# Expert feed-forward: first product of experts 2 to 6 by seven block products in place of eight

## The chip, the cores and the metric

The kernel runs on one core of one Trainium2 chip. A core has five engines with their own instruction queues: PE (TensorE, matrix products), ACT (ScalarE), DVE (VectorE), POOL (GpSimd) and SP (SyncE, which here only starts transfers). PE writes its results to PSUM, of which this stage has eight banks of 128 x 512 floats; ACT and DVE read PSUM, POOL doesn't. Each engine takes its instructions in order and waits on semaphores for the others.

The metric is the device time of one execution in microseconds. Three runs of the kernel before gave 1509.0, 1509.32 and 1512.29 us: median 1509.32. The profile shown is of one more execution, which took 1511.89 us around a span of 1510.1 us from its first instruction to its last.

## The reference, cut to what matters

The model has two layers on 4096 tokens of 256 values in float32. The change lies in the last part, an expert-choice mixture: each of eight experts takes the 1024 tokens that score highest for it, runs them through two matrix products, and adds the result, scaled, to those tokens.

```python
S = sigmoid(xt @ Wg).T                     # 8 x 4096
G, I = top_k(S, 1024)                      # of each expert
ex = xt[I]                                 # 8 x 1024 x 256
hid = gelu(einsum('ekh,ehf->ekf', ex, W1) + b1[:, None, :], approximate=False)
out = (einsum('ekf,efh->ekh', hid, W2) + b2[:, None, :]) * G[..., None]
new_x = zeros_like(xt).at[I.reshape(-1)].add(out.reshape(-1, h))
x = x + layernorm(new_x)
```

W1 is 256 x 1024 for each expert and W2 is 1024 x 256. The first product is thus 1024 tokens x 256 x 1024, with all three sizes even in halves: 2 x 512 tokens, 2 x 128 inputs, 2 x 512 hidden values.

## The kernel before, in words

The mixture is the last stage of the kernel. It works in 16 units `u` of 512 tokens: expert `e = u // 2`, half `q = u % 2` of its tokens. Unit 0 begins at about 1020 us of the profile.

**One unit.** `turn(u, c)` (L2090) transposes the gathered tokens, 128 x 128 at a time, into one PSUM bank (`tp`, two banks) for each half `c` of the 256 inputs, and DVE copies the bank to `xT`. `feed_forward(u)` (L2105) then runs over eight blocks `f` of 128 hidden values: two products of 128 x 128 weights with 128 x 512 tokens (c = 0, 1) add up in one bank `ph` (three banks in turn), and ACT puts the Gelu of it into `hid[:, f, :]` (L2127). Every float32 product is two PE instructions in the profile. Then, for each of four blocks `i` of 128 tokens, eight products give `py` (128 x 256, two banks, L2137). DVE adds the bias to `y` (L2156) and multiplies by the gate (L2157), and POOL starts an indirect transfer that adds the 128 rows of `y` to the tokens' rows in memory, `acc_d` (L2158). There are four `y` buffers. After `i` = 1 and 2 the unit transposes half c = 0 and 1 of the next unit's tokens.

**Weights.** Two experts' weights are held. `load_expert(e + 2)` (L1712) is called when expert e is through: SP loads w1 when the last product that reads the old w1 is done, and w2 likewise.

**The order.** The order of the PE, DVE and ACT instructions is the order in which the program writes them (`manual_schedule`, L1692). POOL's is found by the scheduler up to unit 12, and from there on (L2202) it too is the written one. Transfers that add to `acc_d` are ordered one behind the other, since they write the same tensor; only those of expert 6 are declared independent of each other (`beside_each_other`, L1956).

**The lists.** Which 1024 tokens an expert takes is found while earlier experts run. Searches for the thresholds (of expert 0, of 1, of 2 and 3 together, of 4 to 7 together: a `compare` and ten `tick` each, L1750 and L1764) and the experts' lists (`sort`, `rank`, `chunks`, `places`, `collect`, `gather`, L1877) stand in an agenda. `go_on_with_lists(u, time)` (L2182) is called after each `f` and each `i`; it takes `time` from what the last step is reckoned to cost, and issues the next step when less than 0.3 is left and the step's `behind` allows it. A `gather` makes eight indirect transfers of 128 tokens on POOL (L1928).

**The end.** Before unit 13 POOL is given eight fetches of the last expert's residual rows, `xg` (L2204). Before unit 14 `begin_last` (L2043) reads the sums `acc_d` back: SP brings six blocks of 512 tokens, POOL fetches the last expert's own rows `accg`, both when all transfers of expert 6 have landed. Beside units 14 and 15 the sums of the eight blocks are normalized (statistics on DVE, the power on POOL, L1973, scaling on ACT, L1993) and written out, and at the end the last expert's tokens are written over them by eight transfers (L2032), which wait for all blocks to have been written.

The tiles `x0` to `x3` (128 x 1024 floats each) hold tokens of the first layers, and the mixture doesn't read them before the change.

Of the kernel before, what the change touches and what calls it, by code (L numbers as in the profile page):

```python
# [9 lines left out]
F32 = mybir.dt.float32  # L10
# [9 lines left out]
P = 128  # L20
D = 256
DC = D // P
TB = 512
# [51 lines left out]
def kernel(  # L75
# [1613 lines left out]
    with ExitStack() as st4:  # L1689
# [400 lines left out]
        def turn(u, c, half=None):  # L2090

            if c == 0 and not half:
                xT[u] = wk.tile([P, DC, TB], F32, tag="xT", name="xT")
            e, q = divmod(u, QPE)
            tiles = range(NJ) if half is None else range(half * NJ // 2, (half + 1) * NJ // 2)
            tp = ps.tile([P, NJ, P], F32, tag="tp", name="tp")
            for i in tiles:
                nc.tensor.transpose(tp[:, i, :], lists[e].got[q * NJ + i][:, c * P : (c + 1) * P], ident)  # L2098
                if u == 0 and c == 0 and i == 0:

                    keep_busy(first, 4)
            cols = slice(tiles[0] * P, (tiles[-1] + 1) * P)
            nc.vector.tensor_copy(xT[u][:, c, cols], tp.rearrange("p j t -> p (j t)")[:, cols])  # L2103

        def feed_forward(u):  # L2105
            e, q = divmod(u, QPE)
# [4 lines left out]
            for h in range(TB // n):  # L2111
# [3 lines left out]
                for f in range(FC):  # L2115
                    if not u and not h and f in (FC - 4, FC - 3):
                        turn(0, f - FC + 4, 1)
                    ph = ps.tile([P, n], F32, tag="mm", name="ph", bufs=3)
                    for c in range(DC):
                        nc.tensor.matmul(  # L2120
                            ph,
                            lhsT=w1[:, c, f * P : (f + 1) * P],
                            rhs=xT[u][:, c, h * n : (h + 1) * n],
                            start=(c == 0),
                            stop=(c == DC - 1),
                        )
# [5 lines left out]
                    aside(u, "f", f)  # L2132
            for i in range(NJ):
                k = q * NJ + i
                py = ps.tile([P, D], F32, tag="y", name="py")
                for f in range(FC):
# [4 lines left out]
                        start=(f == 0),  # L2141
                        stop=(f == FC - 1),
                    )
                if u == 1:
                    if i == 2:
                        for c in range(DC):
                            turn(u + 1, c)
                elif i in (1, 2) and u + 1 < NE * QPE:
                    turn(u + 1, i - 1)
# [17 lines left out]
                if e == NE - 2:  # L2167

                    beside_each_other(scatter, summed)
                go_on_with_lists(u, 2.3)  # L2170

        searches = [Search(0), Search(1), Search(2, 3), Search(4, 5, 6, 7)]
        agenda = []
        for search in searches[1:]:
            agenda.extend(search.steps())
            for e in search.es:
                agenda.extend(lists[e].steps())
        left = [0.0]  # L2180

        def go_on_with_lists(u, time):  # L2182
            left[0] = max(left[0] - time, 0.0)
            if agenda and left[0] < 0.3 and agenda[0][1] <= u:
                spent, _, step = agenda.pop(0)
                left[0] += spent
                step()

        first = ps.tile([P, TB], F32, tag="mm", name="idle", bufs=3)
# [9 lines left out]
        for u in range(NE * QPE):  # L2199
# [5 lines left out]
                    last.fetch(xg[:, c, :], x_d, c)  # L2205
            elif u == (NE - 1) * QPE:
                begin_last()
            feed_forward(u)
            if q == QPE - 1 and e + 2 < NE:
                weights.append(load_expert(e + 2))  # L2210

# [33 lines left out]
```

## Time and profile before

| what | value |
| --- | --- |
| median of three runs | 1509.32 us (1509.0 to 1512.29) |
| profiled execution | 1511.89 us, its span 1510.1 us, mean clock granted to PE 0.985 |
| mixture from its first `ph` to the last `py` | 1020.7 to 1498.4 us |
| `ph`, L2120, PE | 544 instructions (480 of 128 x 512, 64 of 128 x 256), 229.6 us busy |
| `py`, L2137, PE | 1024 instructions of 128 x 256, 229.7 us busy |
| Gelu from a bank of 128 x 512, L2127, ACT | 120, 687 ns each |
| copy of a bank of 128 x 512 to `xT`, L2103, DVE | 30, 691 ns each |
| `y`, L2156 and L2157, DVE | 56 each, 420 and 364 ns |
| transfers that add to `acc_d`, L2158, POOL | 56, 1586 ns of POOL each |
| transfers that gather tokens, L1928, POOL | 64, 1041 ns of POOL each |

An entry such as `128x512 f32<-128x512 f32` is partitions x elements and type, of the output and of the input. In a timeline the columns are start, duration, engine, line, operation, output <- input, number of instructions and, in brackets, how long the engine stood before it and what ended that. A duration of several PE instructions is that of the row, so the time from one row's start to the next row's start gives the pace.

### The profile page before, as it was taken

The page shows a single profiled execution, that of the slowest core. Times are in us where ns is not written, and L with a number is a line of the kernel's source. Part 1 is how long each engine was busy: PE and PEld are TensorE (multiplying, and loading weights), DVE is VectorE, ACT ScalarE, POOL GpSimd, SP SyncE. Part 2 cuts the span into 40 slices and gives each one's busy share as a digit, 9 for nine tenths or more (in the row PEclk, how much of TensorE's full clock was granted, in tenths as well). Part 3 has the DMA queues.
Part 4 walks back from the last instruction along what each step waited for, and adds up shares of the span by engine and source line. Part 5 has one row for each costly group of instructions (what it writes and reads, how often), then busy time and mean ns, then how long its engine had stood idle before and what let it go on. Part 6 is the DMA issues. An engine that isn't in the chain of part 4 may idle for free. (4 is left out here: it accounts for less than half of the span.)

```text
span 1510.1 us, 24181 instructions
## 1 busy us (share of the span) xinstructions
PE 1461.7 (97%) x9286; PEld 786.1 (52%) x9286; DVE 876.1 (58%) x2140; ACT 698.2 (46%) x1148; POOL 496.5 (33%) x627
## 2 busy tenths in 40 slices
PE   8999999999899999999999999949999999999996
PEld 4666666667532333332333335517666656665674
DVE  5456654666356599659974877775545631322145
ACT  4244455443456666767676788612211122112143
POOL 4123332222350214322432233413334243242554
PEclk9999999999999999999999999969999999999998
DMA  9400000003324141533154210241324324233364
GB/s 219 132 1 1 1 1 1 1 0 101 103 93 144 52 135 60 179 102 102 47 174 140 71 57 30 75 133 34 101 54 92 67 53 98 50 78 81 64 171 122
DMA packets 91885, 121.58 MB, mean 81 GB/s; under 512 B 24925, under 2 KB 64250, under 8 KB 91642
## 3 DMA queue, kind: packets, MB, share of 16 engines
q1 hardware_dynamic: 70000, 73.09, 15.4%
q0 software_dynamic: 21712, 46.94, 13.3%
q8 instruction: 73, 1.20, 0.3%
q14 instruction: 42, 0.34, 0.1%
q10 hardware_dynamic: 58, 0.01, 0.0%
HBM read 66.90 MB, written 53.12 MB: 79 GB/s over the span
## 5 line engine op out<-in xcount | busy, mean ns | idle before, releaser
L1529 PE MATMUL po<-w,vaug 128*17 128x512 f32 (+1 forms) x2304 | 270.1, 551 | 2.8 <-DVE turned L1579 2.6
L2127 ACT ACTIVATE hid<-ph,mb 128x512 f32<-128x512 f32 (+1 forms) x136 | 89.9, 662 | 340.4 <-PE ph L2120 247.8
L2120 PE MATMUL ph<-xT,w 128*128 128x512 f32 (+1 forms) x544 | 229.6, 574 | 0.3 <-DVE xT L2103 0.3
L2137 PE MATMUL py<-w,hid 128*128 128x256 f32 x1024 | 229.7, 380 | 0.0
L2137 PEld LDWEIGHTS py<-w,hid 128*128 128x128 f32 x1024 | 191.7, 190 | 31.7 <-issue 6.7
L1517 DVE TENSOR_SCALAR w<-sc 128x1024 f32<-128x1024 f32 x152 | 185.1, 1222 | 36.2 <-PE sc L1501 33.8
L1509 ACT ACTIVATE w<-sc 128x512 f32<-128x512 f32 x256 | 152.9, 597 | 113.7 <-ACT w L1513 49.5
L1501 PE MATMUL sc<-q,kT 32*128 32x512 f32 (+1 forms) x2304 | 190.8, 413 | 2.2 <-ACT w L1509 1.0
L1501 PEld LDWEIGHTS sc<-q,kT 32*128 32x128 f32 x2304 | 86.2, 183 | 174.7 <-ACT w L1509 92.1
L2158 POOL DMA_INDIRECT acc_d<-y,idx x56 | 88.8, 1586 | 225.2 <-DVE y L2157 103.2
L2120 PEld LDWEIGHTS ph<-xT,w 128*128 128x128 f32 x544 | 99.8, 190 | 107.4 <-issue 98.3
L1513 ACT ACTIVATE w<-sc 128x512 f32<-128x512 f32 x203 | 120.2, 592 | 0.0
L1515 ACT ACTIVATE w<-sc 128x1024 f32<-128x1024 f32 x104 | 106.7, 1026 | 0.0
L2156 DVE TENSOR_TENSOR y<-py,mb 128x256 f32<-128x256 f32 x56 | 23.5, 420 | 126.7 <-PE py L2137 116.1
L1529 PEld LDWEIGHTS po<-w,vaug 128*17 128x17 f32 x2304 | 41.7, 95 | 95.8 <-issue 72.3
L1928 POOL DMA_INDIRECT got<-tok_d,idx x64 | 66.6, 1041 | 62.9 <-DVE counts L1762 24.5
L2103 DVE COPY xT<-tp 128x512 f32<-128x512 f32 (+1 forms) x34 | 22.2, 659 | 71.1 <-PE tp L2098 62.4
L724 PE MATMUL pg<-nT,wh 128*128 128x512 f32 x128 | 61.4, 612 | 1.5 <-ACT nT L663 1.5
L850 PE MATMUL py<-wo,oT 128*128 128x256 f32 x256 | 61.9, 385 | 0.0
L740 PE MATMUL pv<-wh,nT 128*128 128x512 f32 x128 | 59.7, 592 | 0.0
L850 PEld LDWEIGHTS py<-wo,oT 128*128 128x128 f32 x256 | 47.2, 190 | 17.2 <-issue 9.6
L915 ACT ACTIVATE hid<-ph,vec 128x512 f32<-128x512 f32 x64 | 39.8, 685 | 27.5 <-PE ph L906 27.4
(309 smaller groups left out, 2108.8 us busy)
## 6 DMA issues: line engine op xcount, KB each, us to landing
q<-q_d POOLq DMA_DIRECT2D x16, 1024.0 KB
w<-in_L_ffn_W_dram SPq DMA_DIRECT2D x16, 1024.0 KB
q_d<-parts SPq DMA_DIRECT2D x48, 256.0 KB
kT<-k_d POOLq DMA_DIRECT2D x16, 512.0 KB
k_d<-parts SPq DMA_DIRECT2D x24, 256.0 KB
acc_d<-logits SPq DMA_DIRECT2D x8, 512.0 KB
tok_d<-hg SPq DMA_DIRECT2D x32, 128.0 KB
x<-in_L_attn_x_dram SPq DMA_DIRECT2D x7, 512.0 KB
```

Source lines behind the costliest of these rows:

```text
L850: nc.tensor.matmul(py, lhsT=d["oT"][:, e, :], rhs=wo[:, e, :], start=(e == 0), stop=(e == EC - 1))
L1501: nc.tensor.matmul(sc[:, m * n : (m + 1) * n], lhsT=row["kT"][t][rows, r, (kt + m) * P : (kt + m + 1) * P], rhs=row["q"][qh, t][rows, r, p ...
L1509: nc.scalar.activation(w[:, 0, :], singles[0], AF.Relu)
L1513: nc.scalar.activation(w[:, 1, :], singles[1], AF.Relu)
L1515: nc.scalar.activation(w[:, 2:4, :], pair, AF.Relu)
L1517: nc.vector.tensor_scalar(w[:, 2:4, :], pair, 0.0, None, ALU.max)
L1529: nc.tensor.matmul(po[32 * j : 32 * j + HD + 1, weighed(halves, r)], lhsT=row["v"][:, kt + m, HQ * t + 4 * r + j, :], rhs=w[:, j, m * n : ...
L1928: return nc.gpsimd.indirect_dma_start(out=dst, out_offset=None, in_=rows[:, :], in_offset=self.at_chunk(c), bounds_check=NT - 1, oob_is_er ...
L2120: nc.tensor.matmul(ph, lhsT=w1[:, c, f * P : (f + 1) * P], rhs=xT[u][:, c, h * n : (h + 1) * n], start=(c == 0), stop=(c == DC - 1),)
L2127: nc.scalar.activation(hid[:, f, h * n : (h + 1) * n], ph, AF.Gelu, bias=mb1[:, e * FC + f : e * FC + f + 1])
L2137: nc.tensor.matmul(py, lhsT=hid[:, f, i * P : (i + 1) * P], rhs=w2[:, f, :], start=(f == 0), stop=(f == FC - 1),)
L2158: scatter = nc.gpsimd.indirect_dma_start(out=acc_d[:, :], out_offset=lists[e].at_chunk(k), in_=y, in_offset=None, bounds_check=NT - 1, oob ...
```

## The change

For experts 2 to 6 the first product of both halves of the tokens is made at once, by seven products of blocks in place of eight (the form of Strassen's method that Winograd gave). With the weights' four blocks a (of 128 x 512), the tokens' four blocks b (128 x 512) and sums of them S, T, the seven products are a11 b11, S2 T2, S3 T3, S1 T1, a12 b21, a22 T4 and S4 b22, and the four blocks of the hidden values are sums of these.

- **`weight_sums(e)`**: four additions or subtractions of 128 x 512 on POOL, issued ahead of the `py` of the expert before (for expert 2 ahead of unit 3). S3 takes the place of a21 in w1, the others go to halves of x0 to x3.
- **`token_sums(e, n)`**: four subtractions of 128 x 512 on DVE, after the last transposes of the expert before.
- **`feed_forward_by_seven(e)`**: for each of four blocks f, seven products in four banks. ACT copies the first product to `u2`, DVE makes five additions, and ACT makes four Gelu, three of them from SBUF.
- **`project_back(u, hid)`** is the second half of `feed_forward`, taken out; it runs for both halves of the tokens one after the other, and four `hid` blocks of the two halves are ready at once. Both halves of the next expert's tokens are transposed in the second of them.
- The copies of transposed tokens of experts 2 to 6 go from DVE to ACT.
- `tp` shares the banks of `ph`: five of tag `mm` in place of three and two.
- The agenda: the search for experts 4 to 7 moves ahead of list 3, split around it; `go_on_with_lists` is called 15 times in an expert (7 beside the products, 8 beside `py`) in place of 24, with larger times, and beside the products a step may be held back by `most`.
- The loop over units calls `feed_forward_by_seven(6)`, with both `project_back`, at unit 12. The fetches of `xg` stay written at unit 13 of the loop, and so come behind both halves' `py` and their transfers.

```diff
-            tp = ps.tile([P, NJ, P], F32, tag="tp", name="tp")
+            tp = ps.tile([P, NJ, P], F32, tag="mm", name="tp", bufs=5)
...
-            nc.vector.tensor_copy(xT[u][:, c, cols], tp.rearrange("p j t -> p (j t)")[:, cols])
+            copy = nc.scalar.copy if by_seven(e) else nc.vector.tensor_copy
+            copy(xT[u][:, c, cols], tp.rearrange("p j t -> p (j t)")[:, cols])
+
+        def by_seven(e):
+
+            return 2 <= e < NE - 1
+
+        rooms = [x.rearrange("p j d -> p (j d)")[:, h * TB : (h + 1) * TB] for x in xs[:4] for h in range(2)]
+        seven = dict(zip(("sum0", "T1", "sum1", "T2", "T4", "S1", "S2", "S4"), rooms))
+
+        def weight_sums(e):
+
+            w1, _ = weights[e]
+            (a11, a21), (a12, a22) = ([w1[:, c, h * DFF // 2 : (h + 1) * DFF // 2] for h in range(2)] for c in range(DC))
+            for name, x, y, op in (
+                ("S1", a21, a22, ALU.add), ("S3", a11, a21, ALU.subtract), ("S2", "S1", a11, ALU.subtract),
+                ("S4", a12, "S2", ALU.subtract),
+            ):
+                dst = a21 if name == "S3" else seven[name]
+                nc.gpsimd.tensor_tensor(dst, seven[x] if isinstance(x, str) else x, seven[y] if isinstance(y, str) else y, op)
+
+        def token_sums(e, n):
+
+            (b11, b21), (b12, b22) = ([xT[QPE * e + q][:, c, :] for c in range(DC)] for q in range(QPE))
+            t1, t2, t4 = (seven[name] for name in ("T1", "T2", "T4"))
+            dst, x, y = ((t1, b12, b11), (t2, b22, t1), (b12, b22, b12), (t4, b21, t2))[n]
+            nc.vector.tensor_tensor(dst, x, y, ALU.subtract)
+
+        def turns_within(u):
+
+            e, q = divmod(u, QPE)
+            if u == QPE * NE - 1:
+                return {}
+            turns = {c: (lambda c=c: turn(u + 1, c)) for c in range(DC)}
+            if q == QPE - 1 and by_seven(e + 1):
+                both = [
+                    turns[0], turns[1], lambda: turn(u + 2, 0), lambda: token_sums(e + 1, 0), lambda: turn(u + 2, 1),
+                    *(lambda n=n: token_sums(e + 1, n) for n in (1, 2, 3)),
+                ]
+                return {1: both[0:1], 2: both[1:3], 3: both[3:]}
+            if by_seven(e) and q == 0:
+                return {}
+            return {2: [turns[0], turns[1]]} if u == 1 else {1: [turns[0]], 2: [turns[1]]}
+
+        def feed_forward_by_seven(e):
...
+            HC = FC // 2
+            for f in range(HC):
+                a, b, c, d = (ps.tile([P, TB], F32, tag="mm", name=f"ph{k}", bufs=5) for k in range(4))
+                u2 = seven[f"sum{f % 2}"]
+                c22, c21, c12 = hid[1][:, HC + f, :], hid[0][:, HC + f, :], hid[1][:, f, :]
+                product(a, w1[:, 0, 0:half], b11, True, True, f)
+                nc.scalar.copy(u2, a)
+                product(b, s2, t2, True, True, f)
+                nc.vector.tensor_tensor(u2, u2, b, ALU.add)
+                product(c, s3, t3, True, True, f)
+                nc.vector.tensor_tensor(c22, u2, c, ALU.add)
+                product(d, s1, t1, True, True, f)
+                nc.vector.tensor_tensor(c22, c22, d, ALU.add)
+                product(a, w1[:, 1, 0:half], b21, False, True, f)
+                gelu(0, f, a)
+                if f < HC - 1:
+                    go_on_with_lists(QPE * e, 3.2, 1.5)
+                gelu(1, HC + f, c22)
+                product(c, w1[:, 1, half:DFF], t4, False, True, f)
+                nc.vector.tensor_tensor(c21, u2, c, ALU.add)
+                gelu(0, HC + f, c21)
+                product(d, s4, b22, False, True, f)
+                nc.vector.tensor_tensor(c12, u2, d, ALU.add)
+                gelu(1, f, c12)
+                go_on_with_lists(QPE * e, 3.0)
+            for q in range(QPE):
+                if q == 0 and by_seven(e + 1):
+                    weight_sums(e + 1)
+                project_back(QPE * e + q, hid[q])
...
-                go_on_with_lists(u, 2.3)
+                go_on_with_lists(u, 3.4 if by_seven(e) else 2.3)
...
-            agenda.extend(search.steps())
+            agenda.extend(search.steps() if search is not searches[-1] else ())
             for e in search.es:
                 agenda.extend(lists[e].steps())
+                if e == 2:
+                    agenda.extend(searches[-1].steps()[:4])
+                elif e == 3:
+                    agenda.extend(searches[-1].steps()[4:])
...
-            if agenda and left[0] < 0.3 and agenda[0][1] <= u:
+            if agenda and left[0] < 0.3 and agenda[0][1] <= u and agenda[0][0] <= most:
...
-            feed_forward(u)
+            if u == 3:
+                weight_sums(2)
+            if not by_seven(e):
+                feed_forward(u)
+            elif q == 0:
+                feed_forward_by_seven(e)
             if q == QPE - 1 and e + 2 < NE:
                 weights.append(load_expert(e + 2))
```

More of the change, by code (lines that the diff above doesn't have):

```diff
@@ new lines, in feed_forward_by_seven, with product, gelu @@
+        def feed_forward_by_seven(e):
+            w1, w2 = weights[e]
+            hid = [wk.tile([P, FC, TB], F32, tag="hid", name="hid") for _ in range(QPE)]
+            (b11, b21), (t3, b22) = ([xT[QPE * e + q][:, c, :] for c in range(DC)] for q in range(QPE))
+            t1, t2, t4 = (seven[name] for name in ("T1", "T2", "T4"))
+            half = DFF // 2
+            s3 = w1[:, 0, half:DFF]
+            s1, s2, s4 = (seven[name] for name in ("S1", "S2", "S4"))
+            def product(bank, a, b, start, stop, f):
+                nc.tensor.matmul(bank, lhsT=a[:, f * P : (f + 1) * P], rhs=b, start=start, stop=stop, skip_group_check=not start)
+            def gelu(n, f, src):
+                nc.scalar.activation(hid[n][:, f, :], src, AF.Gelu, bias=mb1[:, e * FC + f : e * FC + f + 1])
+            HC = FC // 2
[27 more added lines that the diff above has]
+                project_back(QPE * e + q, hid[q])
@@ L2117, in feed_forward @@
                         turn(0, f - FC + 4, 1)
-                    ph = ps.tile([P, n], F32, tag="mm", name="ph", bufs=3)
+                    ph = ps.tile([P, n], F32, tag="mm", name="ph", bufs=5)
                     for c in range(DC):
@@ L2132, in feed_forward, with project_back @@
                     aside(u, "f", f)
+            project_back(u, hid)
+        def project_back(u, hid):
+            e, q = divmod(u, QPE)
+            w1, w2 = weights[e]
+            ahead = turns_within(u)
             for i in range(NJ):
@@ L2143, in feed_forward @@
                     )
[L2144 to L2149, printed above, removed]
+                for do in ahead.get(i, ()):
+                    do()
                 gates = lists[e].got[k][:, D + e : D + e + 1]
@@ L2176, with go_on_with_lists @@
         for search in searches[1:]:
-            agenda.extend(search.steps())
+            agenda.extend(search.steps() if search is not searches[-1] else ())
             for e in search.es:
                 agenda.extend(lists[e].steps())
+                if e == 2:
+                    agenda.extend(searches[-1].steps()[:4])
+                elif e == 3:
+                    agenda.extend(searches[-1].steps()[4:])
         left = [0.0]
-        def go_on_with_lists(u, time):
+        def go_on_with_lists(u, time, most=4.0):
             left[0] = max(left[0] - time, 0.0)
-            if agenda and left[0] < 0.3 and agenda[0][1] <= u:
+            if agenda and left[0] < 0.3 and agenda[0][1] <= u and agenda[0][0] <= most:
                 spent, _, step = agenda.pop(0)
@@ L2187, in go_on_with_lists @@
                 step()
-        first = ps.tile([P, TB], F32, tag="mm", name="idle", bufs=3)
+        first = ps.tile([P, TB], F32, tag="mm", name="idle", bufs=5)
         for n, (_, _, step) in enumerate(searches[0].steps() + lists[0].steps()):
```

## The prediction

> **What bounds the kernel now.** I read the page's busy shares first, then a table of stretches for the changed experts, then the timelines of PE and POOL.
>
> ```profile
> PE 1461.7 (97%) x9286; PEld 786.1 (52%) x9286; DVE 876.1 (58%) x2140; ACT 698.2 (46%) x1148; POOL 496.5 (33%) x627
> ```
>
> The same by stretch, for experts 4, 5 and 6 (columns: stretch, its length, busy us of PE, weight loads, DVE, ACT and POOL, clock, DMA share, GB/s):
>
> ```profile
> 1266.14:1325.67 59.53, 59.53 (x244) 38.62 (x243) 14.31 (x40) 11.26 (x17) 20.64 (x17) 1.00 0.33 72
> 1325.67:1385.25 59.58, 59.58 (x244) 38.68 (x243) 14.30 (x40) 11.26 (x17) 20.77 (x17) 1.00 0.33 72
> 1385.25:1442.22 56.97, 56.97 (x211) 38.06 (x210) 8.78 (x21) 10.99 (x16) 29.70 (x25) 1.00 0.35 75
> ```
>
> PE never pauses and has its full clock. Whether it is at its pace shows in unit 13:
>
> ```profile
> 1413.79 13.90 PE L2120 MATMUL ph<-xT,w 128*128 128x512 f32 x32
> 1427.52 7.07 PE L2137 MATMUL py<-w,hid 128*128 128x256 f32 x32
> 1434.43 0.60 PE L2098 MATMUL tp<-ident,got 128*128 128x128 f32 x4
> 1434.87 3.62 PE L2137 MATMUL py<-w,hid 128*128 128x256 f32 x16
> ```
>
> From start to start: 13.73/32 = 0.429 us for an instruction of `ph`, 6.91/32 = 0.216 for one of `py`, 0.44 for four transposes. A block `i` of `py` takes 16 x 0.216 = 3.46. PE is the bound, so work taken from it counts in full until something else is late.
>
> That something could be POOL. It is 33% busy, but the timeline of unit 10 shows how it stands between transfers:
>
> ```profile
> 1342.36 1.01 POOL L1928 DMA_INDIRECT got<-tok_d,idx  x1 [0.30 <-PE py L2137]
> 1344.27 1.62 POOL L2158 DMA_INDIRECT acc_d<-y,idx  x1 [0.89 <-DVE y L2156]
> 1348.91 1.56 POOL L2158 DMA_INDIRECT acc_d<-y,idx  x1 [3.02 <-DVE y L2157]
> 1353.42 1.55 POOL L2158 DMA_INDIRECT acc_d<-y,idx  x1 [2.94 <-issue]
> 1358.01 1.55 POOL L2158 DMA_INDIRECT acc_d<-y,idx  x1 [3.04 <-issue]
> ```
>
> A transfer into `acc_d` can't start until the one before has landed. Their distance is 4.51 to 4.64 us with all `y` long ready (mean of those quoted 4.58; I take 4.55), though POOL is busy for 1.56 of it. Eight hold POOL's queue for 36.4 us, eight gathers for 8 x 1.31 = 10.5: 47 of 59.5 us.
>
> **The Trainium skill.** "Perfetto Trace Analysis", Identifying the Most-Contended Engine, calls matmul busy time a bad measure, since matmuls are pipelined; hence the pace above, which agrees with a full PE here. "DMA: Bandwidth & Descriptors", Rules for kernel authors, says an accumulating transfer beside another access of the same bytes must wait for the earlier one's semaphore; the 4.5 us steps are that wait. "VectorE: DVE Perf Modes", What auto-detection actually checks, says `tensor_tensor` gets a faster mode only with 16-bit data; the trace agrees: 1224 ns for 1024 elements (L2002).
>
> **The change, part by part.** Zero is the end of the last transpose ahead of an expert's products, unless said otherwise.
>
> 1. Fewer products: 32 become 28, each two instructions: 8 x 0.429 = 3.43 us less on PE for each expert, **-17.2** for five. One PE wait of 0.56 for `counts` in unit 5 goes with its cover (**-0.6**). Transposes and `py` stay.
>
> 2. Steady f loop. Seven products last 6.01. DVE: five additions of 128 x 512. No such row exists; L2156 takes 420 ns for 256, and 256 more at the slope of L2002's engine (1/0.96 ns) give 0.69, with 0.03 to the next: 3.6. ACT: one copy at 586 ns (L1352) and four Gelu at 687: 3.3. Nearest waits: ACT copies the first product behind the last Gelu of the f before, so by 2.25 after f's start; DVE then has `u2` at 3.0, the first `c22` at 3.75, the second at 4.5. The third bank is written again at 4.29 and the fourth at 5.15, which need those two. So cost 0, with about 0.6 us of slack. A list step of DVE takes from its 2.4 us of pauses and this slack; `rank`, the longest there, fits. No `tick` falls there (counting the agenda through, ticks 3 to 9 of the last search fall beside `py` of units 4 and 5). With additions of 0.9 the slack is gone.
>
> 3. Head of an expert. Last copy by ACT 0.2 to 0.8, T2 from 0.9 to 1.6, T3 2.3, T4 3.1, then the last `y` 3.8. PE's second product needs T2: 1.65 in place of 0.86, **0.8** lost. DVE then does `u2`, `c22`, `c22` by 6.0; the products shifted by 0.8 need them at 5.1 (first `c22`, there at 5.3): 0.2 to 0.3 more. So 1.1 at the least. After units 7, 9 and 11 a step `places` (1.3 us DVE, L1894 twice) stands behind that `y`: 1.7; after unit 5 a `sort`: 1.5. Sum 1.1 + 1.5 + 3 x 1.7 = **+7.7** (ends 4 and 11).
>
> 4. POOL. An addition of 128 x 512 has no row; 730 ns for 256 (L364) and 2353 for 1024 (L588) put it at 1.27, so four take **5.1** (ends 4.5 and 7). For each expert POOL's queue now holds 36.4 + 10.5 + 5.1 = 52 us, with one transfer some 2 us slower beside a load of w2 (1265.21 to 1271.29 took 6.1): 54 of a period of about 57. All eight transfers now fall in 28 us of `py`, where PE makes a `y` each 3.46. Four `y` buffers cover that, if POOL starts on time: transfers 0 to 3 land at 4.5 x (1 to 4) behind their start, and `y` 4 to 7 are wanted at 17.5, 21, 25, 29 after the products' end. In experts 4 to 6 the gathers are asked for in the second f and done in time. In 2 and 3 the agenda puts `gather` behind the last f: POOL then does 10.5 of gathers and 5.1 of sums first and starts transfer 0 about 17 after the products' end, where `y` 0 was ready at 4.3. It lands at 21.5, and `y` 4 is 4 us late; the second `py` bank hides all but 1.1 us, the next two buffers add 0.7, and the rest of the lateness reaches DVE's queue, the next rank or tick on PE and the next head: about 2.7 an expert, **+5.4** (ends 0 and 14).
>
> 5. Ticks beside `py` of units 4 and 5: a tick is 3.1 us of DVE (rows of L1790 to L1762 at 1159.51), with `y` 3.85 against PE's 3.46; the next tick's small product on PE waits for it: **+1.5** (0.5 to 3).
>
> 6. The end. The fetches of `xg` move from unit 13's middle to behind the last transfer of expert 6. Before:
>
> ```profile
> 1426.28 1.01 POOL L1928 DMA_INDIRECT xg<-x_d,idx  x1 [0.30 <-issue]
> ...
> 1448.09 1.08 POOL L1928 DMA_INDIRECT accg<-acc_d,idx  x1 [3.03 <-DMA acc_d<-y,idx]
> ...
> 1453.17 1.06 POOL L1973 TENSOR_TENSOR rsc<-vec,mhalf 128x4 f32<-128x4 f32 x1
> ...
> 1490.60 1.16 POOL L2032 DMA_INDIRECT out_dram<-xg,idx  x1 [0.55 <-issue]
> ...
> 1502.16 1.04 POOL L2032 DMA_INDIRECT out_dram<-xg,idx  x1 [0.80 <-DVE xg L2028]
> ```
>
> Against unit 14's start (1442.22) POOL is free at 2.9; eight fetches end at 13.4, four of `accg` at 18.7, where they ended at 10.95. The first power is 7.8 later, and behind it ACT's scaling. POOL's pauses from 1453 to 1479 add up to 5.4, which leaves 2.4; DVE's wait for the later `accg` adds about 1.3. In unit 15 ACT has a Gelu and two scalings, 1.73, for each f of PE's 1.72, so it makes nothing good; the last block is stored that much later, and the eight closing transfers wait for it, POOL being 12.2 of 12.6 us busy there. **+3.8** (ends 1 and 5.5).
>
> Other moves: the copies to ACT free 2.8 us of DVE an expert; ACT has over 40 us to spare. Five shared banks are never short, since an f starts with the first four's predecessors read. SP's loads wait for the same products as before and lie within `py`.
>
> Sum: -17.2 - 0.6 + 7.7 + 5.4 + 1.5 + 3.8 = **+0.6**, a span of 1510.7 against 1510.1. The profiled execution lies 2.6 above the median; carried to that, 1509.9, so **1510**.
>
> **Rivals.** A change under 0.2%, 3 us, can't be told from none here.
>
> - *Faster*: the list of losses is only the head (5.5 at its bare 1.1 each), ticks 0.5 and an end of 2 to 3.8, because POOL catches up: its idle time in experts 4 and 5, 39 us of each 59.5 by busy share, speaks for it; the 4.55 us holds speak against. -17.8 + 5.5 + 0.5 + 2 to 3.8 = -9.8 to -8: 1499.5 to 1501.5. With part of POOL's loss, up to 1506.
> - *Slower*: POOL's queue becomes the bound. With d us from transfer to transfer an expert holds it for 8d + 10.5 + 5.1 + 2. That is the forecast's period of some 57 at d = 4.9, and at d = 5.3 it is the 60.0 of before (1145.10 to 1385.25 for experts 2 to 5). From there on it decides: experts 3 to 5 gain nothing, expert 2 loses 1.9 (-3.4 + 1.1 + 2.7 + 1.5), expert 6, whose transfers aren't chained, gains 1.7, the end loses 3.8: +4, 1513; at d = 5.5 three times 1.6 more, 1518. For it: 5.6 and 6.1 stand in the trace beside loads of weights, and now transfers lie closer. Against: all others are within 0.2 of 4.5.
> - *DVE bounds the f loop*: additions of 1.0 would cost about 0.3 an f, 6 us in 20, on top of the forecast: 1516. The slope of L2002 speaks against.
>
> That seven products are not made in place of eight is excluded by the code.
>
> **How the numbers follow.** The forecast, losses as priced, 0.36, with its own range 1506.5 to 1512.5; faster 0.35; slower 0.29 (POOL 0.2, DVE 0.09). The range cuts about a tenth at either end: 1500 to 1517.
>
> **What would show it.** Right: `ph` instructions of the five experts fall from 320 to 280; PE, never idle before, shows waits for DVE's T at each head of about 1 us; POOL's first transfer of experts 2 and 3 starts some 12 us behind its `y`, and DVE's `y` waits for transfers there; unit 14 starts 2 to 4 us earlier than before, and from there to the end takes 71 to 72 in place of 67.9. Wrong: an order of POOL in which sums or gathers lie elsewhere (the scheduler's until unit 12), additions far from 0.69 or 1.27, `acc_d` distances other than 4.5, or an end as long as before.

## The result, and the profile after

The changed kernel takes 1513.85 us (median of 20 runs, 1507.53 to 1521.6) where the kernel before takes 1509.16 beside it (20 runs, 1508.2 to 1512.66). The ratio is 1.0031, 95% interval 1.0019 to 1.0044: slower by 0.3%. The profiled execution took 1520.59 us around a span of 1518.7, 6.7 above the median, so what its profile shows at the end is a bad case of something that varies.

The busy shares of the page, after:

```profile
PE 1451.6 (96%) x9246; PEld 780.0 (51%) x9246; DVE 945.5 (62%) x2240; ACT 718.5 (47%) x1188; POOL 525.3 (35%) x647
```

PE has its 40 instructions less, and is 10 us less busy. The table of stretches, after, for experts 2 to 6 and for the end (units 14 and 15); the columns are those of the table before:

```profile
1147.73:1211.25 63.52, 59.77 (x245) 37.77 (x243) 48.05 (x118) 15.70 (x25) 23.25 (x18) 0.97 0.28 63
1211.25:1268.47 57.22, 56.59 (x239) 37.03 (x238) 30.59 (x75) 15.37 (x25) 26.29 (x20) 1.00 0.34 73
1268.47:1325.54 57.07, 56.41 (x238) 37.08 (x236) 28.31 (x60) 15.47 (x25) 27.95 (x21) 1.00 0.39 79
1325.54:1382.49 56.95, 56.32 (x237) 37.14 (x236) 27.83 (x60) 15.47 (x25) 27.61 (x21) 1.00 0.35 75
1382.49:1438.54 56.05, 55.40 (x227) 36.13 (x226) 25.55 (x46) 13.81 (x22) 23.11 (x17) 1.00 0.31 60
1438.54:1518.70 80.16, 59.44 (x201) 38.54 (x199) 37.50 (x140) 26.35 (x48) 47.19 (x51) 0.89 0.54 148
```

Experts 4 and 5 took 59.53 and 59.58 before and gain 2.5 and 2.6. Experts 2 and 3 and the end took, before:

```profile
1145.10:1204.00 58.90, 58.34 (x223) 38.52 (x220) 37.11 (x98) 11.26 (x17) 20.04 (x15) 1.00 0.34 73
1204.00:1266.14 62.14, 62.14 (x279) 39.20 (x278) 20.08 (x59) 11.53 (x18) 21.74 (x17) 1.00 0.30 69
1442.22:1510.10 67.88, 56.13 (x201) 37.07 (x199) 38.06 (x140) 26.90 (x48) 37.18 (x43) 0.94 0.59 159
```

Expert 2 doesn't gain. Experts 2 and 3 have to be taken together, though, since steps of the lists moved: PE has 22 instructions more than before in expert 2 (245 against 223) and 40 fewer in expert 3 (239 against 279). With the starts of the stages, found in PE's timelines, the whole difference of the two spans can be laid out (before, after, difference, in us):

| stage | before | after | difference |
| --- | --- | --- | --- |
| unit 1 | 31.62 | 35.67 | +4.0 |
| unit 3 | 33.46 | 32.07 | -1.4 |
| expert 2 | 58.90 | 63.52 | +4.6 |
| expert 3 | 62.14 | 57.22 | -4.9 |
| experts 4 and 5 | 119.11 | 114.02 | -5.1 |
| expert 6 | 56.97 | 56.05 | -0.9 |
| units 14 and 15 | 67.88 | 80.16 | +12.3 |
| all | 1510.1 | 1518.7 | +8.6 |

So there is the gain, and three losses in three places. PE's timeline, after, at the start of expert 6, answers to that of unit 13:

```profile
1382.49 1.02 PE L2158 MATMUL ph<-xT,w 128*128 128x512 f32 x2
1384.15 1.10 PE L2158 MATMUL ph<-x,x 128*128 128x512 f32 x2 [0.63 <-DVE x L2129]
```

The second product starts 1.66 us after the first where 0.86 is the pace: the bare head costs 0.8. POOL's timeline, after, beside the second half of expert 5, answers to that of unit 10:

```profile
1357.73 1.62 POOL L2249 DMA_INDIRECT acc_d<-y,idx  x1 [1.89 <-DVE y L2248]
1362.39 1.56 POOL L2249 DMA_INDIRECT acc_d<-y,idx  x1 [3.04 <-issue]
1366.90 1.54 POOL L2249 DMA_INDIRECT acc_d<-y,idx  x1 [2.95 <-issue]
```

The distances are 4.66 and 4.51, as before. Now the three losses.

**Unit 1.** On POOL, after, the sums of expert 2's weights, written ahead of unit 3, stand behind unit 1's first transfer:

```profile
1073.36 1.62 POOL L2249 DMA_INDIRECT acc_d<-y,idx  x1 [0.30 <-issue]
1074.44 1.84 POOL L2122 TENSOR_TENSOR x<-w 128x512 f32<-128x512 f32 x1
1076.36 1.26 POOL L2122 TENSOR_TENSOR w<-w 128x512 f32<-128x512 f32 x1
1077.59 1.27 POOL L2122 TENSOR_TENSOR x<-x,w 128x512 f32<-128x512 f32 x1
1078.93 1.29 POOL L2122 TENSOR_TENSOR x<-w,x 128x512 f32<-128x512 f32 x1
```

and on DVE, at the same time, a tick:

```profile
1076.77 0.89 DVE L1793 TENSOR_TENSOR tried<-best,bits 128x16 int32<-128x16 int32 x1
1077.69 2.78 DVE L1755 TENSOR_TENSOR ge<-by_e,tried 128x224 bf16<-128x224 f32 x2
```

These take 0.17 and 0.69 in the ticks on either side. PE waits for the tick's `counts`, and its next block is slow besides:

```profile
1081.18 0.17 PE L1769 MATMUL parts<-counts,all_b 128*128 128x16 bf16 x1 [2.40 <-DVE counts L1762]
1081.20 5.39 PE L2232 MATMUL py<-w,hid 128*128 128x256 f32 x16
1086.43 0.17 PE L1769 MATMUL parts<-counts,all_b 128*128 128x16 bf16 x1
```

2.40 of waiting and 5.23 for a block that took 3.54 just before: 4.1. What makes the block slow is PE's granted clock: cut into stretches of 1 us, the profile has it at 0.50 from 1081.6 to 1085.0 and at 1.00 ahead of that and after it.

**The head of expert 2.** DVE's timeline, after, has the third tick of a search behind the last `y` of unit 3, ahead of the first sum of results:

```profile
1151.72 1.30 DVE L1755 TENSOR_TENSOR ge<-by_e,tried 128x224 bf16<-128x224 f32 x4
...
1154.06 0.68 DVE L2171 TENSOR_TENSOR x<-x,ph 128x512 f32<-128x512 f32 x1
```

and PE waits for its fourth bank and is then slow for two products (its clock is 0.50 from 1156.7 to 1160.1):

```profile
1152.01 1.02 PE L2158 MATMUL ph<-xT,w 128*128 128x512 f32 x2
1155.58 1.12 PE L2158 MATMUL ph<-x,w 128*128 128x512 f32 x2 [2.55 <-DVE hid L2173]
1156.55 1.76 PE L2158 MATMUL ph<-xT,x 128*128 128x512 f32 x2
```

**The end.** POOL's timeline, after, with the instructions shown of before:

```profile
1441.70 1.08 POOL L1928 DMA_INDIRECT xg<-x_d,idx  x1 [0.30 <-issue]
...
1456.27 1.01 POOL L1928 DMA_INDIRECT accg<-acc_d,idx  x1 [0.31 <-issue]
1457.30 1.22 POOL L1973 TENSOR_TENSOR rsc<-vec,mhalf 128x4 f32<-128x4 f32 x1
...
1499.10 1.16 POOL L2032 DMA_INDIRECT out_dram<-xg,idx  x1 [0.55 <-issue]
```

Up to the first power all is as step 6 has it (18.8 us after unit 14's start; 18.7 was predicted). But from there to the first closing transfer it is 41.8 us, where before it was 37.4 and the prediction reckoned with some 33.4, as pauses were to take up 4 us of the delay. The chain that ended last, after, says what lies there (start, us, what):

```profile
1467.52 5.69 DMA out_dram<-back_w
1473.26 13.06 DMA back_w<-acc_d
1486.34 1.41 DVE stc L1969 x4
```

The read-back of block 7 takes 13 us. It starts when block 1 has been stored, and that is now the time at which the stores of blocks 2 and 3, which add to memory, are started too (1472.84). ACT's Gelu stands behind the scaling of such a block, so PE stops for 8.57 us in unit 15's second product and is slow after it (its clock is 0.50 from 1487.8 to 1498.0).

### The profile page after: what moved, and what is told of

Read it like the earlier page. It is cut to its first block, busy times and chain, and to the rows that moved or that the text cites. A ratio compares the mean times of both kernels' runs of the same rounds, so it can differ in the third digit from the quotient of the medians.

```text
span 1518.7 us, 24330 instructions
## 1 busy us (share of the span) xinstructions
PE 1451.6 (96%) x9246; PEld 780.0 (51%) x9246; DVE 945.5 (62%) x2240; ACT 718.5 (47%) x1188; POOL 525.3 (35%) x647
## 5 line engine op out<-in xcount | busy, mean ns | idle before, releaser
L2232 PE MATMUL py<-w,hid 128*128 128x256 f32 x1024 | 233.5, 386 | 9.1 <-ACT hid L2215 8.9
L2215 ACT ACTIVATE hid<-ph,mb 128x512 f32<-128x512 f32 (+1 forms) x56 | 34.6, 623 | 128.3 <-PE ph L2208 108.1
L2208 PE MATMUL ph<-xT,w 128*128 128x512 f32 (+1 forms) x224 | 86.4, 538 | 0.3 <-DVE xT L2104 0.3
L2104 ACT COPY xT<-tp 128x512 f32<-128x512 f32 x20 | 11.2, 586 | 121.2 <-PE parts L1833 59.4
L2158 PE MATMUL ph<-xT,w 128*128 128x512 f32 x120 | 63.0, 607 | 0.0
L2208 PEld LDWEIGHTS ph<-xT,w 128*128 128x128 f32 x224 | 41.0, 190 | 37.6 <-issue 33.5
```

The source lines that it names most:

```text
L2158: nc.tensor.matmul(bank, lhsT=a[:, f * P : (f + 1) * P], rhs=b, start=start, stop=stop, skip_group_check=not start)
L2208: nc.tensor.matmul(ph, lhsT=w1[:, c, f * P : (f + 1) * P], rhs=xT[u][:, c, h * n : (h + 1) * n], start=(c == 0), stop=(c == DC - 1),)
L2232: nc.tensor.matmul(py, lhsT=hid[:, f, i * P : (i + 1) * P], rhs=w2[:, f, :], start=(f == 0), stop=(f == FC - 1),)
```

## The experiments

The kernel before was timed beside each run on the same chip; ratios are to it. The theory when they were made: the change saves what step 1 says, and loses it in the three places above, by separate causes. The rivals: POOL's queue or DVE's load costs PE time all along; the shared PSUM tag does; the end is long because unit 14 now comes closer behind expert 6's transfers.

| run | ratio, 95% interval | in its profile |
| --- | --- | --- |
| changed kernel | 1.0031 (1.0019 to 1.0044) | unit 1 35.67, expert 2 63.52, end 80.16 |
| before, late fetches | 1.0050 (1.0032 to 1.0067) | end 77.78 |
| fetches between units 12 and 13 | 0.9997 (0.9982 to 1.0012) | end 76.45 |
| fetches ahead of unit 12's transfers | 0.9969 (0.9955 to 0.9983) | end 67.82 |
| eight rooms | 0.9991 (0.9982 to 1.0000) | end 72.89 |
| sums held back | 1.0010 (0.9996 to 1.0023) | unit 1 31.58 |
| before, sums added | 1.0031 (1.0016 to 1.0046) | unit 1 34.59 |
| tick moved | 0.9995 (0.9980 to 1.0010) | expert 2 59.14 |
| three edits | 0.9927 (0.9914 to 0.9940) | span 1499.7 |
| three edits, no weight sums | 0.9928 (0.9914 to 0.9943) | span 1500.1 |
| three edits, tokens earlier | 0.9903 (0.9887 to 0.9920) | span 1492.6 |

A profile is one execution. Those of the fetches between units 12 and 13 (1517.16 us, median 1509.77), of eight rooms (1513.40, median 1508.35) and of the tick moved (1515.55, median 1510.75) were caught 5 to 7 us above their medians, that of the sums held back (1509.47, median 1513.22) 4 below. Spans also hold up to 4 us from ahead of the mixture, which begins at 1020.7 in both kernels, at 1021.0 with three edits and at 1017.0 in the last run. So the stages tell where time goes, and the ratios how much it is on the whole.

### The end: the order of the fetches, in the kernel before

```diff
-            elif u == (NE - 1) * QPE - 1:
+            elif u == (NE - 1) * QPE:
                 for c in range(NC):
                     last.fetch(xg[:, c, :], x_d, c)
-            elif u == (NE - 1) * QPE:
                 begin_last()
```

> The kernel before with one thing changed: the eight fetches of x for the last expert are issued behind unit 13's four transfers in place of ahead of them. Step 6 of the prediction alone, without any seven-product part. Prediction as made: from the start of unit 14 to the end 71 to 72 us in place of 67.9, median 1512 to 1513. Theory now (late fetches, and then the read-backs of the last two blocks fall into the accumulating stores): 72 to 80 us, varying by several us between executions, median 1513 to 1518. Rival (the order of these fetches is hidden, and the end of the changed kernel is long because expert 6's first products are shorter): 67.5 to 69 us, median within 1 us of 1509.2.

Ratio 1.0050, 7.4 us on the median, and in the profile 77.78 for units 14 and 15. So step 6 is real and alone costs twice what was predicted on the median, and 9.9 in this profile. The read-back of the last two blocks, then two stores, then the statistics of block 7 (SP's, POOL's and DVE's timelines of this run):

```profile
1471.20 3.15 SPq L1979 DMA_DIRECT2D back_w<-acc_d  x2
```

```profile
1473.18 1.98 POOL L2000 DMA_DIRECT2D out_dram<-back_w  x2
```

```profile
1484.01 1.41 DVE L1969 BATCH_NORM_STATS2 stc<-back_w 128x6 f32<-128x256 f32 x4 [6.19 <-DMA back_w<-acc_d]
```

### The end: the fetches back between the transfers of units 12 and 13

```diff
+                if q == 1 and e == NE - 2:
+                    for c in range(NC):
+                        last.fetch(xg[:, c, :], x_d, c)
                 project_back(QPE * e + q, hid[q])
...
-            elif u == (NE - 1) * QPE - 1:
-                for c in range(NC):
-                    last.fetch(xg[:, c, :], x_d, c)
```

> The changed kernel with one thing put back: the eight fetches of x for the last expert (xg) are issued on GpSimd between the transfers of unit 12 and those of unit 13, as before, in place of behind all eight transfers of expert 6. Theory (the end is long because those fetches stand behind expert 6's transfers): from the start of unit 14 to the end 67.5 to 70 us in place of 80.2, the read-back of blocks 6 and 7 issued some 28 us after the start of unit 14, nothing changed before it; the median falls by 4 to 8 us to about 1506 to 1510, and its spread from 14 us to about 5. Rival (the end is long for another reason, such as a shorter time to the end of expert 6's transfers): the stretch stays at 75 to 80 us and the median within 1.5 us of 1513.9.

It is 0.3% faster than the changed kernel, which the theory allowed. But in the profile, of an execution above this kernel's median, the end is still 76.45, and the spread stays at 13 us, so the theory in this form was wrong: this place is better and still not good. POOL's timeline of this run:

```profile
1427.21 1.08 POOL L1928 DMA_INDIRECT xg<-x_d,idx  x1 [0.30 <-issue]
...
1437.85 1.62 POOL L2252 DMA_INDIRECT acc_d<-y,idx  x1 [0.30 <-issue]
...
1443.51 1.54 POOL L2252 DMA_INDIRECT acc_d<-y,idx  x1 [0.30 <-issue]
1448.12 1.08 POOL L1928 DMA_INDIRECT accg<-acc_d,idx  x1 [3.07 <-DMA acc_d<-y,idx]
```

Before, the products of unit 13 stood between the two halves' transfers and gave POOL the time for these fetches. Now both `project_back` follow each other, the fetches take 10.6 us from 1427.21 to 1437.85, and the transfers of unit 13 run one behind the other with nothing to wait for but POOL. The fetch of `accg`, which waits for the last of them to land, starts 9.4 us after unit 14's start (1438.75), where before it was 5.9. "Behind expert 6's transfers" was not the point: both places tried so far, behind these transfers and between them, make the end late.

### The end: the fetches ahead of all transfers of expert 6

```diff
+            if e == NE - 2:
+                for c in range(NC):
+                    last.fetch(xg[:, c, :], x_d, c)
             for q in range(QPE):
                 if q == 0 and by_seven(e + 1):
...
-            elif u == (NE - 1) * QPE - 1:
-                for c in range(NC):
-                    last.fetch(xg[:, c, :], x_d, c)
```

> The changed kernel with the eight fetches of x for the last expert issued on GpSimd ahead of all of expert 6's transfers, directly behind the gathers for expert 7, where GpSimd stood idle for 7.8 us in the profile. Theory (expert 6 by seven products has no room between the transfers of units 12 and 13; put between them, the fetches took 10.6 us and made unit 13's transfers late, which is why that kernel's end stayed at 76.5 us): expert 6's first transfer some 3 us later, its last one unchanged, the last expert's first fetch of sums some 6 us after the start of unit 14, and from there to the end 67.5 to 70 us in place of 80.2; median 6 to 9 us below the changed kernel's, ratio 0.997 to 0.999. Rival (the end is long whatever the order, since unit 14 starts closer behind expert 6's transfers): 75 us or more, ratio 1.000 or more.

As expected: 67.82, and 0.9969. POOL's timeline of this run: the first transfer of expert 6 starts 8.1 us after the products' end in place of 4.9, the last isn't late, and the `accg` fetch comes 5.9 us after unit 14's start (1435.68):

```profile
1413.88 1.62 POOL L2252 DMA_INDIRECT acc_d<-y,idx  x1 [0.30 <-issue]
...
1436.97 1.55 POOL L2252 DMA_INDIRECT acc_d<-y,idx  x1 [1.31 <-DVE y L2251]
1441.56 1.08 POOL L1928 DMA_INDIRECT accg<-acc_d,idx  x1 [3.04 <-DMA acc_d<-y,idx]
```

Expert 6 itself takes 57.31 in place of 56.05. PE waits 1.1 us there for DVE's second `y`, in this run and in the three below that have the same early fetches, and in no other. So it is the price of this edit. How it comes about isn't shown: by the profile that `y` waits for PE's `py`, and not for a transfer.

### The end: the delay, or what it collides with?

```diff
             room_back.extend(wk.tile([P, NJ, D], F32, tag="back", name="back") for _ in range(2))
+            room_back.extend(xs[t] for t in range(2))
```

> The changed kernel with eight rooms for the read-backs in place of six (the first two tiles of tokens, free after expert 6's products), so that blocks 6 and 7 are read back together with the others at the start of unit 14 and don't fall beside the accumulating stores. The fetches of x stay behind expert 6's transfers. Theory (the end is long because the late fetches push the stores of the first blocks, and with them the read-back of blocks 6 and 7, which then runs beside other stores): no wait of VectorE of 5 us or more for back tiles after the start of unit 15, TensorE's stop before unit 15's second product gone, from the start of unit 14 to the end 69 to 73 us in place of 80.2; median 4 to 7 us below the changed kernel's, ratio 0.998 to 1.001. Rival (it is the fetches' delay as such that reaches the end): 77 to 81 us, ratio 1.003.

72.89, in the range of the theory, with the fetches as late as in the changed kernel; the ratio falls to 0.9991. So of the 12.3 us in the changed kernel's profile 7.3 go with the late read-back of blocks 6 and 7, and 5.0 remain with the delay (step 6 had 3.8). By the ratios, over all executions, eight rooms gain 6.0 us (0.40%). The 5.0 aren't the delay alone: with all read-backs at once PE waits 2.19 us in unit 14 for `accg`, which it didn't in the changed kernel, and eight rooms weren't tried in the kernel before. How the read-back comes to be late can be read from all these profiles together: the time from the row of that pair of read-backs to the row of the next pair of stores on POOL, and to the statistics of block 7 on DVE:

| kernel | to the stores | to block 7's statistics |
| --- | --- | --- |
| before; before with sums | 4.4; 4.4 | 8.2; 8.3 |
| early fetches; three edits; with tokens earlier | 4.0; 4.6; 4.3 | 7.8; 8.5; 8.2 |
| changed kernel; tick moved | 2.6; 2.6 | 16.1; 14.8 |
| sums held back; fetches between; before with late fetches | 2.8; 2.2; 2.0 | 12.7; 15.7; 12.8 |

In the first two rows DVE didn't wait for the block, so its transfer was shorter than that. Between 2.8 and 4.0 us of lead the read-back goes from passing ahead of the stores to arriving as if held up by them. A race decided by 1 to 2 us would also fit the spreads: 13 to 14 us in four of the five kernels of the last two rows and 9 in the fifth (six runs), 3 to 8 in the other edited ones, eight rooms (7.9) among them, and 4 to 9 in the kernel before. That it is the stores which hold it up is read from this table and not tried by itself, nor which part of the transfers' way they share; the last two fetches of `accg` stand just ahead of these stores in every run and aren't told apart from them.

### Unit 1: the sums held back

```diff
-                nc.gpsimd.tensor_tensor(dst, ...)
+                one = nc.gpsimd.tensor_tensor(dst, ...)
+                if e == 2 and name == "S1":
+                    after_all(one, [scaled_last[2]])
...
-                nc.vector.tensor_scalar(y, y, gates, None, ALU.mult)
+                scaled_last[u] = nc.vector.tensor_scalar(y, y, gates, None, ALU.mult)
```

> The changed kernel with the sums of expert 2's weights held back on GpSimd until unit 2's last result is made, so that they can't run beside unit 1's comparisons on VectorE. Theory (these sums slow VectorE's comparisons, which read two SBUF tiles, and so make TensorE wait): unit 3 starts at about 1111.6 us in place of 1115.7, the comparisons of the tick in unit 1 take 0.35 us each in place of 1.39, everything later is 4 us earlier; the median falls by 3.5 to 4.5 us to about 1509.5 to 1510.5. Rival (the 4 us come from the shared PSUM tag with five buffers, or from the slower first matmuls after any pause): unit 3 still starts at 1115 to 1116 us and the median stays within 1 us of 1513.9.

Unit 1 takes 31.58 again. DVE's timeline of this run, the comparisons of the same tick:

```profile
1075.13 0.69 DVE L1755 TENSOR_TENSOR ge<-by_e,tried 128x224 bf16<-128x224 f32 x2
```

Unit 3 starts at 1109.78, 5.9 earlier; 1.8 of that was there before unit 1 and 4.1 is unit 1. The ratio of 1.0010 doesn't part the two expectations well, the stage does. The run with the early fetches has the sums where the changed kernel has them and the same wait of PE (2.43 us), but its clock stays at 1.00, and unit 1 takes 34.27: of the 4.1, some 1.4 hang on the clock.

### Unit 1: the sums alone, in the kernel before

```diff
+        def weight_sums(e):
...
+            if u == 3:
+                weight_sums(2)
             feed_forward(u)
```

> The kernel before with one thing added: the four additions of weights for expert 2 on GpSimd, written where the changed kernel writes them, into tiles that nobody reads (so the result is that of the kernel before). It stands on GpSimd where it stands in the changed kernel, behind unit 1's first transfer. Theory (GpSimd's additions slow the comparisons on VectorE, and TensorE's pause then makes its next matmuls slower): the two comparisons of that tick take 2.8 us together in place of 0.7, unit 1 takes 34 to 36 us in place of 31.6, nothing else changes; ratio 1.0015 to 1.003. Rival (the loss needs the shared PSUM tag or the seven-product code): unit 1 takes 31.6 us, ratio 0.9993 to 1.0007.

Unit 1 takes 34.59, 3.0 more, and all other stages of the mixture are within 0.2 of the kernel before; the ratio is 1.0031 (1.0016 to 1.0046), which is 4.7 us. PE's clock stayed at 1.00 in the profile; that it falls in other executions would account for the rest, which isn't shown. So the loss needs neither the shared PSUM tag nor the new code, only the four additions at that place. But it wasn't the comparisons that suffered this time. DVE's timeline of this run:

```profile
1071.96 4.06 DVE L2168 TENSOR_SCALAR y<-y,got 128x256 f32<-128x256 f32 x1
```

and POOL's:

```profile
1071.60 3.05 POOL L2114 TENSOR_TENSOR x<-w 128x512 f32<-128x512 f32 x2
1074.05 1.82 POOL L2114 TENSOR_TENSOR x<-x,w 128x512 f32<-128x512 f32 x1
```

The multiplication by the gate, 0.35 us elsewhere, ends 0.15 after POOL's third addition. A few tenths decide which DVE instruction is caught.

### The head of expert 2: the tick moved

```diff
-                go_on_with_lists(u, 3.4 if by_seven(e) else 2.3)
+                if u != 3 or i < 2:
+                    go_on_with_lists(u, 3.4 if by_seven(e) or u == 3 else 2.3)
```

> The changed kernel with the third tick of the search for experts 2 and 3 moved from behind unit 3's last result (so at the head of expert 2 on VectorE) to unit 3's second block, with the second tick one block earlier too; all later steps keep their places. Theory (the tick holds up the first two sums of results of expert 2, which costs more than the 1.1 us that the prediction gave this head): expert 2 takes 59 to 60 us in place of 63.5, unit 3 grows by at most 1 us, the median falls by 3 to 4 us. Rival (the head of expert 2 costs 4 us by itself, as the others would if more stood on VectorE): expert 2 stays at 63 us, and the median within 1 us of 1513.9.

Expert 2 takes 59.14 (4.4 less), unit 3 32.25 (0.2 more). The table of stretches of this run, for expert 2:

```profile
1148.21:1207.35 59.14, 57.83 (x245) 37.38 (x243) 45.17 (x110) 15.37 (x25) 23.38 (x18) 1.00 0.29 68
```

PE's clock there is 1.00 again, where it was 0.97. So the tick costs 4.4 and the head without it 0.8 like the others. Of the 4.4, some 1.5 hang on the clock: in the run with the sums held back PE waits 2.55 us at this head too, its clock stays at 1.00, and expert 2 takes 61.99.

### All three, and what is left

The edits of the early fetches, the held-back sums and the moved tick together:

> The changed kernel with three edits together: the fetches of x ahead of expert 6's transfers, the sums of expert 2's weights held back until unit 2's last result, the tick away from the head of expert 2. If the three causes are apart from each other and are all that the change lost, the stages add up: unit 3 starts at 1111.6 less the run's own offset, then 32.2, 58.5 to 59.5, 57.2, 57.1, 57.0, 56.1 and 68 us, which is a span of 1498 us; ratio to the kernel before 0.991 to 0.993. If they overlap (one delay hides in another) the span is 1503 or more and the ratio 0.995 to 0.998.

A span of 1499.7 and 0.9927. That is 1.7 above the 1498 of the expectation: 0.2 is the run's own offset before unit 1, and expert 6 takes 57.48, 1.4 more than in the changed kernel, with the early fetches. Apart from that price the removals add up, so the causes are apart. This version beats both kernels. The same without the sums of weights (S1, S2 and S4 replaced by blocks of the weights, S3 left unsubtracted, so this kernel leaves out a part of the computation):

```diff
-            s1, s2, s4 = (seven[name] for name in ("S1", "S2", "S4"))
+            s1, s2, s4 = w1[:, 1, half:DFF], w1[:, 0, 0:half], w1[:, 1, 0:half]
...
-                    weight_sums(e + 1)
```

> As the run with the three edits, and without the sums of weights: the three products that take a sum of weights take a block of the weights itself (part of the computation is left out), so GpSimd has 20 additions of 1.27 us less. Step 4 of the prediction (these additions make the transfers of experts 2 and 3 late, and this reaches TensorE): 4 to 6 us faster than with them, most of it in experts 2 and 3. Theory now (their delay of the transfers is taken up by VectorE's and GpSimd's slack): within 1 us of the run with the three edits in every stage.

0.9928, no difference. The tables of stretches for expert 3, first of the three edits, then of this run:

```profile
1203.16:1260.39 57.23, 56.60 (x240) 37.04 (x239) 30.72 (x75) 15.39 (x25) 26.18 (x20) 1.00 0.33 72
```

```profile
1203.51:1260.73 57.22, 56.59 (x239) 37.09 (x238) 30.66 (x75) 15.37 (x25) 19.91 (x16) 1.00 0.34 75
```

POOL (the fifth busy time) has 6.3 us less to do, and the stage is 0.01 shorter; expert 2 is 0.2 shorter. Last, the heads:

```diff
-                return {1: both[0:1], 2: both[1:3], 3: both[3:]}
+                first = 1 if u == 3 else 0
+                return {first: both[0:1], first + 1: both[1:3], first + 2: both[3:]}
```

> As the run with the three edits, and with the transposes, the copies and the sums of the tokens of experts 3 to 6 one block earlier in the last unit of the expert before (those of expert 2 stay). It measures what is left of the heads in step 3 of the prediction. If the heads of experts 3 to 6 cost what they show (TensorE waits 0.63 us for the token sum ahead of the second product, 0.8 us with the slower start of the matmul behind it), experts 3 to 6 take about 0.8 us less each, 3.2 us in all, and the ratio goes from 0.9927 to 0.9905 to 0.992. Rival (the wait only moves: the sums taken earlier on VectorE delay the results of that block and the transfers behind them): the four experts together change by less than 1 us.

0.9903, the fastest kernel here, though its interval overlaps that of the three edits; the stages tell them apart. Experts 3 to 6 take 56.25, 57.15, 56.11 and 56.29 in place of 57.23, 57.06, 56.96 and 57.48: 2.9 less. PE's waits from unit 3 to the end of expert 6 in this run:

```profile
PE py L2240 <- DVE y L2255: 0.9, 1, 0.9
PE ph L2163 <- DVE hid L2178: 0.8, 1, 0.8
PE ph L2163 <- DVE x L2133: 0.6, 1, 0.6
```

The first goes with the early fetches in expert 6. One head is left, that of expert 2 (0.6). Expert 4 gains nothing: there a `y` on DVE stands 2.04 us for a transfer, the sums behind it are late, and PE waits 0.8. So the rival holds for one expert of four.

## Why the prediction was right and wrong

The forecast was 1510 and no measurable change; it is 1513.85, inside the range, and 0.31% slower, which is more than no change. That it lies so near is in part luck: unit 14 starts 3.7 us earlier than before, where 2 to 4 were predicted, but only because 5.4 us of step 4 that never came make room for 4.1 in unit 1 and for the 4.4 of a tick that weren't foreseen. Where both mechanism and size held, and where not:

- **Step 1** held. Expert 5 goes from 59.58 to 56.95: 3.43 less for eight instructions, 0.8 more for the head.
- **Step 2** held: within the products PE waits only in the heads. The additions took 684 to 687 ns on DVE (0.69 priced) and 1.27 on POOL (1.27 priced).
- **Step 3** had a sum near the truth, +7.7 against 5 x 0.8 + 4.4 = 8.4, from wrong terms. A `places` step or a `sort` behind the last `y` was to add 0.4 to 0.6 to four heads; it added nothing. What was missed is the tick at the head of expert 2, 4.4 in place of nothing. The agenda had been counted through for the ticks of the last search only, and the head of expert 2 taken as bare.
- **Step 4** failed, +5.4 where leaving the sums out gains nothing. Its first half came out: in the changed kernel the first transfer of expert 2 starts 14.3 us after the products' end (17 predicted), and DVE's `y` waits 8.8 us in all for transfers. What failed is the step from a late `y` to PE: neither the 1.1 and 0.7 us priced at the `py` banks nor "the rest of the lateness reaches DVE's queue, the next rank or tick on PE and the next head" shows as a wait of PE in the changed kernel. With other waits gone one does, 0.8 once, in the fastest kernel.
- **Step 5**: 0.7 measured, 1.5 priced.
- **Step 6** was right in place and chain up to the first power, and undersized: +3.8 against some 5.0 for the delay, 7.4 on the median in the kernel before, and 12.3 in this profile, both with the late read-back. The link that failed is "the last block is stored that much later": a shift by 4 us was carried through unchanged to the last store, where the shifted read-back and the stores no longer keep their order.
- **Not in the prediction at all**: +4.1 in unit 1. The prediction named the order of POOL as the scheduler's until unit 12, as something that would make it wrong, and put no price on it.

PE's wait of 0.56 in unit 5 is gone, as step 1 had it. With the measured terms the sum for the two profiles is -17.2 - 0.6 + 8.4 + 0.7 + 12.3 + 4.1 = +7.7, against +8.6; the last 0.9 isn't placed. Of the rivals, neither slower one occurred (POOL's queue as the bound, DVE as the bound of the f loop): the chained transfers of experts 2 to 5 stand 4.7 apart in the mean, where 5.3 was needed, and beside the products PE waits in the heads alone. The kernel is slower by other causes. The faster rival is nearest to what the seven products themselves cost: heads at 1.1 (0.8 measured) and no loss by POOL. With the three causes removed it is 0.9927 of 1509.16, so 1498, near the faster rival's 1499.5 to 1501.5, though that was worked out with other terms.

## What to carry to other kernels

When a stage is reordered, list for each engine what the old order put between its steps: here the products of one half gave POOL the room for fetches, and the merged order had none, in either of the two obvious places. Follow a shift to the next place where two transfers or two engines meet, and compare their lead there (here 4 us) with the shift, before carrying it through as a constant. An instruction that a scheduler may place is part of the change wherever its inputs allow it to run, and has to be priced beside whatever its neighbour engine does there.

## What the runs showed of the hardware that wasn't expected

An addition on GpSimd can stop VectorE for longer than itself. The Trainium skill, "SBUF — State Buffer", Who interferes with whom, says that GpSimd's pair of ports is also VectorE's second pair, that some of VectorE's instructions need it (those with two inputs in SBUF, for one), and that whichever engine comes first keeps it for a whole instruction while the other stands still. The traces agree, and show more: several additions issued one behind the other held one VectorE instruction through most of three of them (4.06 us for 0.35), and which one it was changed with some tenths of a us. The same additions beside experts 3 to 6 cost nothing that the stages show (57.23 and 57.22 us for expert 3 with and without them).

After a pause TensorE is sometimes slow, and not always. After 2.40 us of waiting a block took 5.23 in place of 3.54 us; after 2.77 in the kernel before with sums it took 3.77. The granted clock parts the two: 0.50 behind the first pause, 1.00 behind the second. In all these profiles it stands at 0.50 for 3.41 us or a multiple of that (6.83, 10.24) before it is 1.00 again, and within a run these stretches start on one grid of 3.41 us: 1081.60, 1156.70 and 1487.79 in the changed kernel lie 22 and 97 steps apart. Twelve pauses of PE between 2.1 and 2.8 us can be laid on their run's grid. The eight that have 2.30 us or more within one step were all followed by half the clock; the four that have at most 1.92 us within one step were not, and the longest of all, 2.77, lies across a boundary and is one of these. So here the place of a pause on the grid decided, beside its length. This is read from the traces, and no run moved a pause on purpose.
